# Attention kernel on one core: rows fetched as columns in one transfer a set, two additions split or moved, one reciprocal in halves

## Chip, cores, metric

The kernel runs on one core of a Trainium2 chip. The metric is the device time of one execution in microseconds (us): the median of several runs. Five engines are named here: PE (TensorE, matrix products), DVE (VectorE, elementwise work), ACT (ScalarE, copies, exponentials and sums with a bias), POOL (GpSimd, elementwise work beside DVE) and SP (SyncE, which issues most DMA transfers).

## What is computed

Eight images of 512 channels and 32 x 32 positions go through two attention blocks, all in float32:

```python
# layer 0: norm over 32 groups, 8 heads of 64 channels, softmax over positions
h = group_norm(x, norm_w, norm_b)
q, k, v = split(einsum('oc,bchw->bohw', qkv_w, h) + qkv_b)      # 8 heads
attn = softmax(einsum('bhnd,bhmd->bhnm', q, k) / sqrt(64))
o = einsum('bhnm,bhmd->bhnd', attn, v)
x = x + einsum('oc,bchw->bohw', proj_w, o) + proj_b

# layer 1: norm over the whole image, one head, softmax over 1024 positions
nf = norm(x) * gn_gamma + gn_beta
q, k, v = wq @ nf + bq, wk @ nf + bk, wv @ nf + bv
attn = softmax(q^T k * 512 ** -0.5)
out = v attn^T
x = x + wo @ out + bo
```

## The kernel before

Work goes image by image ("batch" 0 to 7), layer 0 and then layer 1, with the products of the next batch's layer 0 mixed in. Most 512- and 1024-wide products are Strassen products: `strassen` (from L640) and relatives compute a product of 2 x 2 blocks with seven block products. They need sums of blocks of both factors (S1 to S4 and T1 to T4), which DVE or POOL makes ahead of time, and sums of the results, which DVE adds from the PSUM banks as each is full. A bank that was not yet read can't be filled again, so an addition that is late keeps PE waiting. Some products apply the scheme twice (`twice` at L1503, `two_of` at L1795); their factors' sums have names with `_twice`.

Order. The order of PE, ACT and DVE is the order in which the program is written. Generators stand for products and give control back after each block product ("step"); `at_steps` runs them and calls given functions ("hooks") at numbered steps. So where a hook stands decides what is in front of what in DVE's queue. SP and POOL are ordered by the framework's scheduler. An engine works through its queue in order, and a DMA issue that has to wait holds everything behind it on the issuing engine.

Weights. Sums of weights that each batch needs are made in the first batch and stored to DRAM (`stored_...`, L247, L566), then loaded again by each later batch. Three large buffers (`wpool`) hold the weights in turn: the tile of v's weights (`w_v`, loaded at L220, its sums made at L195) takes the one that the product of wo and wv (`wvo`) had.

Vectors. The biases of the combined weights come out of PE as rows: class `Rows` (from about L730) multiplies vectors with weights into one PSUM bank, in which chunk cc of the input channels has its row at partition 32 cc (and a second row 16 further on, for sets of two). `store` (L749) copies the bank with ACT and stores all 128 rows to DRAM by SP; `fetch` (L755) loads each row back as a column of 128 partitions x 4, by one SP transfer for each row (8 for a set of two, 4 for a set of one); `add` (L765) adds the four chunks' columns on DVE (L769, L770). There are three sets: v and q, fetched ahead of batch 0 (L1926), and bias0, stored and fetched within batch 0 (L1031).

The places that the change touches, and what stands around them:

- `make_v` for batch 0 (PE L682): its first factor is `w_v`. ACT copies the first banks (L459) to `u_v`, DVE adds (L716). Before it PE makes `ps_k` (L667), which ACT copies with a bias (L697).
- The score blocks of layer 1. `twice("S4", ...)` and `twice("A22", ...)` run together, a step of one and a step of the other in turn. Each step is a group of four matmuls (L1512) into one of four banks, and a DVE addition `p<-ps_l,p` or `p<-ps_s,p` (L1522) that frees the bank. At step 3 a hook `c22(1)` (L1567) adds two whole score tiles of 128 x 1024 in SBUF (`with_p5`, L1565) and ACT takes their exponential (L1486). POOL adds up exponentials beside that (`add_up`, L1483), and then makes `B_p_twice` (L518).
- The values of layer 1. `four_of` for two chunks (PE L1676), then `two_of` (PE L1806, DVE L1812), with `done_values` behind each bank (DVE L1692, L1695). A hook at step 7 makes the four sums `S_v_twice` (`halve_v`, `sums_a`, L511) that `two_of` uses. POOL makes `A_v_twice` and DVE `B_p_twice` of other quarters.
- The end of layer 0 in the last batch. `done` in `project` (L1250 to L1287): behind the first banks of the two products, DVE takes a reciprocal of the last softmax sums (`one_over`, L847, 128 x 512) and divides (`divide`, L1018), then adds the other product's bank (L1273) and makes the remaining T sums (`combine2`, L1068). PE's `ps_p` (L667) needs the bank.

Of the kernel before, what the change touches and what calls it, by code (L numbers as in the profile page):

```python
# [37 lines left out]
FP = mybir.dt.float32  # L38
AF = mybir.ActivationFunctionType
ALU = mybir.AluOpType  # L40
# [6 lines left out]
P = 128  # L47
C = 512
NC = C // P
N = 1024  # L50
NT = N // P
HALF = 512
# [13 lines left out]
def two_attention_blocks(  # L66
# [18 lines left out]
    nc = tc.nc  # L85
    B = x.shape[0]

    const = ctx.enter_context(tc.tile_pool(name="const", bufs=1))
    tpool = ctx.enter_context(tc.tile_pool(name="t", bufs=36))
    wpool = ctx.enter_context(tc.tile_pool(name="w", bufs=3))  # L90
    dram = ctx.enter_context(tc.tile_pool(name="dram", bufs=1, space=bass.MemoryType.DRAM))
    upool = ctx.enter_context(tc.tile_pool(name="u", bufs=5))
    onepool = ctx.enter_context(tc.tile_pool(name="one", bufs=1))
    accpool = ctx.enter_context(tc.tile_pool(name="acc", bufs=2))
# [7 lines left out]
    def tile2(name):  # L102
        return tpool.tile([P, 2, HALF], FP, tag="t", name=name)
# [8 lines left out]
    def piece(ts, cc, half):  # L112

        return ts[cc // 2][half][:, cc % 2, :]
# [173 lines left out]
    def room(name, n=-1):  # L288

        return spares[n] if spares else banks("s", f"ps_{name}")[:, 0, :]  # L290
# [204 lines left out]
                quarter[f"{i + 1}{j + 1}"] = part[:, k, n * 2 * P : (n + 1) * 2 * P]  # L495
        return quarter

    def sums_a(q, t, engine=nc.vector):

        t = t if len(t.shape) == 2 else flat(t)  # L500
        n = t.shape[1] // 4
        for i in range(4):
            part = t[:, i * n : (i + 1) * n]
            if len(q["A11"].shape) == 3:
                part = part.rearrange("p (u o) -> p u o", u=2)
            q[f"S{i + 1}"] = part
        for i, x, y, op in [
            (1, "A21", "A22", ALU.add), (2, "S1", "A11", ALU.subtract),
            (3, "A11", "A21", ALU.subtract), (4, "A12", "S2", ALU.subtract),
        ]:  # L510
            engine.tensor_tensor(q[f"S{i}"], q[x], q[y], op)  # L511
        return q

    def sums_b(q, ts, engine=nc.vector):
# [217 lines left out]
    class Rows:  # L732
# [16 lines left out]
        def store(self):  # L749
            row = tile2(f"row_{self.name}")[:, 0, :]  # L750
            nc.scalar.copy(row, self.ps)
            self.rows = dram.tile([P, C], FP, tag=self.name, name=f"rows_{self.name}")
            nc.sync.dma_start(self.rows, row)

        def fetch(self):  # L755
            self.columns = const.tile(
                [P, self.n, NC, NC], FP, tag=f"c_{self.name}", name=f"c_{self.name}"
            )
            for i in range(self.n):
                for cc in range(NC):  # L760
                    nc.sync.dma_start(
                        self.columns[:, i, cc, :],
                        self.rows[cc * (P // NC) + i * (P // NC // 2)].rearrange("(o p) -> p o", p=P),
                    )

        def add(self, i, name):

            t, c = const.tile([P, NC], FP, tag=name, name=name), self.columns[:, i]
            nc.vector.tensor_tensor(c[:, :2, :], c[:, :2, :], c[:, 2:, :], ALU.add)  # L769
            nc.vector.tensor_tensor(t, c[:, 0, :], c[:, 1, :], ALU.add)  # L770
            made[name] = t
            return t
# [72 lines left out]
    def one_over(ps, name):  # L845
        inv = accpool.tile([P, HALF], FP, tag="inv", name=f"inv_{name}")[:, : ps.shape[1]]
        nc.vector.reciprocal(inv, ps)  # L847
        return inv
# [15 lines left out]
    def flat(t):  # L864
        return t.rearrange("p h n -> p (h n)")
# [76 lines left out]
    def layer0(bs, qs, ks, b, norm_next):  # L942
# [4 lines left out]
        hooks = {}  # L947
# [22 lines left out]
        accs, sums, invs, spreads = {}, {}, {}, {}  # L970
# [45 lines left out]
        def divide(pair, g, inv):  # L1016
            part = piece(os, pair, g)
            nc.vector.tensor_tensor(part, part, inv, ALU.mult)  # L1018

        units = [(pair, g, kt) for pair in ORDER for g in range(2) for kt in range(NT)]  # L1020
        ps = {}
# [5 lines left out]
        if b == 0:  # L1027
            w.finish()
            p0 = waiting[-1]

            def bias0():  # L1031
                rows = Rows([(bias_0, p0.moving)], 1, "bias0", room("bias0"))
                rows.store()
                rows.fetch()
                throughs[:] = [rows]

        hooks = {8: [lambda: score(0)], 9: [lambda: score(1)]}
# [15 lines left out]
        else:  # L1053
            hooks = {n + 10: more for n, more in hooks.items()}
            at_steps(pairs_qk_twice(w, twice_a[0], 1, bs, twice_b, qs, ks, b), hooks)
        last = norm_next is None
# [131 lines left out]
        for i in range(2, len(units) + 2):  # L1188
# [8 lines left out]
            name = f"0_{b}_{pair}_{g}"  # L1197
# [15 lines left out]
        if b == 0:  # L1213
            rows, = throughs
# [5 lines left out]
        if not last:  # L1220
# [3 lines left out]
            hooks = {  # L1224
                3: [lambda n=n: combine2(n, 0) for n in range(1, 5)],
                6: [lambda: folded(end)],
                12: [
                    lambda: sum_couple(couple, [room("sum", g) for g in range(2)]),
                    lambda: copy_couple(couple, 0), lambda: copy_couple(couple, 1), gather_couple,
                ],  # L1230
                14: [lambda: one_over_couple(couple, [nc.sync, nc.scalar])],
                16: [held_couple],
# [17 lines left out]
        def project(w, c):  # L1250
            def done(i, half, bank, u):
                chunk = c + 2 * i
                x = piece(xs, chunk, half)

                def add():
                    nc.vector.scalar_tensor_tensor(  # L1256
                        x, bank if u is None else u, bias[:, chunk : chunk + 1], x, ALU.add, ALU.add
                    )
                    due.append(lambda: norm.moments(chunk, half, i == half))
                    if (i, half, c) == (1, 0, 1):  # L1260
                        ready.halve("B21")


                first = last and i == half == 0
                if first and c == 0:
                    ps_sum, total = spares[0], tile_u(f"total_0_{b}")
                    add_keys(end, [1], ps_sum)
                    nc.scalar.copy(total, ps_sum)
                    combine1()
                    combine2(2, 0)  # L1270
                    combine2(3, 0)
                if u is not None:
                    nc.vector.tensor_tensor(u, bank, u, ALU.add)  # L1273
                if not first:
                    add()
                    return
                later.append(add)
                if c == 0:
                    invs[end] = one_over(total, f"0_{b}_{end}_1")
                    divide(end, 1, invs[end])  # L1280
                else:

                    held(flat(accs[end, 1]), f"acc_0_{b}_{end}", flat(accs[end, 1]))
                    for n, k in [(2, 1), (3, 1), (4, 0), (4, 1)]:
                        combine2(n, k)
                    for more in later:
                        more()  # L1287

            return strassen(by_channels(w, c, comb), done, f"p_0_{b}_{c}")

        w = next_weight().parts[0]
        hooks = {} if last else {2 * n - 3: [lambda n=n: combine2(n, 1)] for n in range(2, 5)}
# [31 lines left out]
    def attention1(xs, norm, ready, b, at_values):  # L1324

        last = b + 1 == B
# [144 lines left out]
        ps = [[[tile2(f"p_1_{b}_{j}{k}{i}") for i in range(2)] for k in range(2)] for j in range(2)]  # L1471
# [87 lines left out]
            done(1, 0)  # L1559
            yield  # L1560

        def with_p5(i, j, k):

            to, other = ps[j][k][i], ps[1][k][1] if i == 0 else ps[0][k][1]
            nc.vector.tensor_tensor(to, to, other, ALU.add)  # L1565

        def c22(k):  # L1567
            with_p5(1, 1, k)
            exp_of(ps[1][k][1])
# [58 lines left out]

        twice_v, twice_p = {}, {}

        def halve_v(name, engine):
            q = {
                f"A{i + 1}{j + 1}": v_parts[j][name][:, :, i * P : (i + 1) * P]
                for i in range(2) for j in range(2)
            }
            twice_v[name] = sums_a(q, tile2(f"{name}_v_twice_{b}"), engine)

        def halve_p(name, engine):
            q = {
                f"B{i + 1}{j + 1}": p_parts[i][name][:, :, j * 2 * P : (j + 1) * 2 * P]  # L1640
                for i in range(2) for j in range(2)
            }
            ts = [tile2(f"{name}_p_twice_{b}_{i}") for i in range(2)]
            sums = [t[:, i, :].rearrange("p (u q) -> p u q", u=2) for t in ts for i in range(2)]
            twice_p[name] = sums_b(q, sums, engine)

        if not last:
            halve_v("A12", nc.gpsimd)
        at_steps(
            together(  # L1650
                twice("S4", "B22", "oo", 0, 1, False, True), twice("A22", "T4", "ss", 1, 0, False, True)
            ),
            {3: [lambda: c22(1)], 5: [] if last else [lambda: halve_p("B22", nc.gpsimd)]},
        )

        for n in range(1, 5):
# [14 lines left out]
        invs, later = [], []  # L1671
# [87 lines left out]
        hooks = {n * 2 - 3: [lambda n=n: finish_values(n)] for n in range(2, 5)}  # L1759
# [64 lines left out]

        hooks[3].append(sums)
        hooks[6] = [lambda: halve_p("B21", nc.vector)]
        hooks[7] = [lambda: halve_v("S4", nc.vector)]
        for n, more in at_values.items():
            hooks.setdefault(n, []).extend(more)
        at_steps(in_turn(together(four_of(0), four_of(1)), two_of()), hooks)  # L1830
# [18 lines left out]
    made, throughs, over = {}, [], []  # L1849


    with tc.manual_schedule(engines={PE, ACT, DVE}):
# [71 lines left out]
        })  # L1924
        bs = combine.parts
        for rows in throughs:  # L1926
            rows.fetch()
        for b in range(B):
            if 0 < b < B - 1:
                ahead = [norm0(load_x(b + 1, nc.sync), b + 1)]  # L1930
# [430 lines left out]
```

## Time and profile before

| | |
|---|---|
| median of 3 runs | 2820.49 us (2820.47 to 2820.8) |
| the profiled execution | 2819.71 us |
| its span, first to last instruction | 2818.0 us |
| granted TensorE clock, mean | 0.999 |
| DMA traffic | 246.45 MB, mean 87 GB/s |

How to read the profile. All durations come from one profiled execution, whose own time is 1.7 us above its span. The page gives the busy time of each engine, the chain of work that ended last, and groups of equal instructions. "PEld" is PE's weight load, which runs beside matmuls. The waits view lists, for each engine and line, what ended its idle time: the total in us, how often, and the longest. The timeline gives one line for an instruction or a run of them: start in us, duration, engine, line, operation, output<-inputs, the shape, the count, and in brackets the idle time before it with what ended it. A "SPq" or "ACTq" line is the issue of a DMA by that engine, not the transfer. A time over a group (x2) covers all of the group.

### The profile page before, as it was taken

To read this page: it belongs to the slowest core of one execution; us is meant where nothing else is said; L and a number is where in the kernel's file an instruction comes from. 1 tells how busy PE (TensorE), PEld (TensorE's weight loads), DVE (VectorE), ACT (ScalarE), POOL (GpSimd) and SP (SyncE) were. 2 spreads that over 40 slices of the span, in tenths; PEclk is the share of its full clock that TensorE was granted. 3 is DMA by queue.
4 is the path that set the end of the run, shared out by engine and by line. 5 is a ranking of instruction groups with operands and counts; after the bars stand their busy time and mean duration, and the time that the engine had idled before them with its cause. 6 is when DMAs were issued, how large, how long until landed. Compare 5 with 4: busy or idle time off the path is not lost.

```text
span 2818.0 us, 39402 instructions
## 1 busy us (share of the span) xinstructions
PE 2805.0 (100%) x15688; PEld 1586.0 (56%) x15688; DVE 2113.7 (75%) x2891; ACT 1172.3 (42%) x1761; POOL 377.7 (13%) x388
## 2 busy tenths in 40 slices
PE   9999999999999999999999999999999999999999
PEld 5535765357653576435764466734667346673375
DVE  5777697766977678776787767777777777767877
ACT  3364224643246332563325533255332653326622
POOL 0001220012100230002400024000240002400021
PEclk9999999999999999999999999999999999999999
DMA  7524132231313313233131331312313132121001
GB/s 252 201 53 132 42 123 79 75 107 63 114 64 87 105 53 112 68 91 114 67 107 43 91 124 57 109 50 85 123 56 108 50 104 104 64 80 62 25 16 39
DMA packets 83575, 246.45 MB, mean 87 GB/s; under 512 B 21784, under 2 KB 22584, under 8 KB 76984
## 3 DMA queue, kind: packets, MB, share of 16 engines
q1 hardware_dynamic: 73768, 209.75, 22.9%
q10 hardware_dynamic: 9616, 34.11, 3.8%
q8 instruction: 125, 2.05, 0.3%
q14 instruction: 66, 0.54, 0.1%
HBM read 186.97 MB, written 33.03 MB: 78 GB/s over the span
## 4 chain that ended last, share of the span: by engine, by line
PE 92%; DVE 6%; issue 1%; DMA 1%; SPq 0%; ACT 0%; POOL 0%; DVEq 0%; ACTq 0%; POOLq 0%
PE s L979 15%; PE ps_o L998 15%; PE ps_v L682 7%; PE ps_o L1676 7%; PE ps_p L667 7%; PE ps_l_qk L904 5%; PE ps_l L1512 4%; PE ps_s L1495 4%; PE ps_s_qk L897 4%; PE ps_l_v L682 3%; PE ps_l_q L667 3%; PE ps_s L1512 3%; PE ps_o_qk L897 3%; PE ps_s_v L925 2%; PE ps_s_q L1370 2%; PE ps_s_two L1806 2%
## 5 line engine op out<-in xcount | busy, mean ns | idle before, releaser
L833 ACT ACTIVATE p<-s 128x1024 f32<-128x1024 f32 x512 | 523.9, 1025 | 328.9 <-PE s L979 322.8
L835 DVE TENSOR_TENSOR acc<-acc,p 128x1024 f32<-128x1024 f32 x384 | 469.1, 1222 | 101.0 <-ACT p L833 92.5
L998 PE MATMUL ps_o<-p,v 64*64 64x512 f32 x4096 | 528.7, 589 | 0.0
L979 PE MATMUL s<-c_q,c_k 64*64 64x512 f32 x3584 | 465.1, 590 | 0.0
L998 PEld LDWEIGHTS ps_o<-p,v 64*64 64x64 f32 x4096 | 156.6, 133 | 282.8 <-issue 278.3
L979 PEld LDWEIGHTS s<-c_q,c_k 64*64 64x64 f32 x3584 | 134.7, 133 | 253.2 <-issue 236.1
L528 POOL TENSOR_TENSOR B_twice<-x 128x512 f32<-128x512 f32 x16 | 20.4, 1274 | 1352.1 <-DVE x L1256 1351.9
L1676 PE MATMUL ps_o<-t_p,s_v 128*128 128x512 f32 x384 | 168.2, 594 | 0.0
L835 DVE TENSOR_TENSOR acc<-p,p 128x1024 f32<-128x1024 f32 x64 | 78.2, 1223 | 79.4 <-ACT p L833 79.4
L1486 ACT ACTIVATE p<-p,factor 128x512 f32<-128x512 f32 (+1 forms) x112 | 85.3, 780 | 116.1 <-DVE p L1522 91.4
L1500 ACT COPY p<-ps_s 128x512 f32<-128x512 f32 x96 | 53.1, 588 | 174.4 <-PE ps_s L1495 174.4
L1676 PEld LDWEIGHTS ps_o<-t_p,s_v 128*128 128x128 f32 x384 | 72.3, 190 | 91.3 <-issue 89.2
L1522 DVE TENSOR_TENSOR p<-ps_l,p 128x512 f32<-128x512 f32 x136 | 89.8, 682 | 40.0 <-PE ps_l L1512 39.7
L459 ACT COPY u_v<-ps_v 128x512 f32<-128x512 f32 x48 | 28.1, 586 | 210.1 <-PE ps_v L682 191.2
L667 PE MATMUL ps_p<-t_p,w_p 128*128 128x512 f32 x256 | 112.7, 592 | 0.6 <-DVE u_p L1273 0.6
L1522 DVE TENSOR_TENSOR p<-ps_s,p 128x512 f32<-128x512 f32 x112 | 74.8, 684 | 37.7 <-PE ps_s L1512 37.7
L682 PE MATMUL ps_v<-w_v,t_again 128*128 128x256 f32 x448 | 99.0, 379 | 0.0
L373 POOL TENSOR_TENSOR rstd<-rstd,minus_half 128x4 f32<-128x4 f32 (+1 forms) x16 | 12.8, 800 | 605.5 <-DVE rstd L372 605.5
L682 PE MATMUL ps_v<-w_v,x 128*128 128x256 f32 x384 | 88.6, 385 | 3.4 <-DMA w_v<-in_s_v 3.4
L682 PEld LDWEIGHTS ps_v<-w_v,t_again 128*128 128x128 f32 x448 | 85.1, 190 | 11.6
L667 PE MATMUL ps_p<-o,w_p 128*128 128x512 f32 x192 | 86.7, 593 | 0.0
L667 PEld LDWEIGHTS ps_p<-t_p,w_p 128*128 128x128 f32 x256 | 48.6, 190 | 62.2 <-issue 58.4
(508 smaller groups left out, 5148.7 us busy)
## 6 DMA issues: line engine op xcount, KB each, us to landing
x<-in_x SPq DMA_DIRECT2D x92, 512.0 KB, 6.4
w_qk<-stored_qk SPq DMA_DIRECT2D x14, 1792.0 KB, 7.1
w_wqk<-stored_wqk SPq DMA_DIRECT2D x8, 1792.0 KB, 7.2
fold<-acc SPq DMA_DIRECT2D x56, 256.0 KB, 3.1
qk_twice<-stored_qk_twice ACTq DMA_DIRECT2D x28, 512.0 KB, 6.1
w_wvo<-stored_wvo SPq DMA_DIRECT2D x8, 1792.0 KB, 8.3
out<-x SPq DMA_DIRECT2D x28, 512.0 KB, 4.7
w_v<-stored_v SPq DMA_DIRECT2D x7, 1792.0 KB, 7.5
```

Source lines behind the costliest of these rows:

```text
L667: nc.tensor.matmul(bank, w[a][:, k, c * P : (c + 1) * P], bs[b][:, k, :], start=fresh and k == 0, stop=k == 1, skip_group_check=True,)
L682: nc.tensor.matmul(bank[:, u * 2 * P : (u + 1) * 2 * P], bs[b][:, k, n * P : (n + 1) * P], w[a][:, k, :], start=fresh and u == k == 0, sto ...
L833: nc.scalar.activation(p, s, AF.Exp, scale=factor)
L835: nc.vector.tensor_tensor(acc, first, p, ALU.add)
L897: nc.tensor.matmul(bank[:, i * 2 * P : (i + 1) * 2 * P], parts[a][x], twice_b[v][y], start=start and i == 0, stop=True, skip_group_check=True,
L904: nc.tensor.matmul(bank, of(i, a)[:, k, :], bs[v][:, k, :], start=start and k == 0, stop=k == 1, skip_group_check=True,)
L979: nc.tensor.matmul(s[cols, j, :], ks[pair][k0 // HALF][rows, k0 % HALF : k0 % HALF + HD], qs[pair][g][rows, :], start=True, stop=True,)
L998: nc.tensor.matmul(o[cols, half, :], vs[kt][rows, c0 : c0 + HD], p[rows, j, :], start=kt == 0, stop=kt == NT - 1,)
L1495: nc.tensor.matmul(bank, bs[v][:, k, t * P : (t + 1) * P], q_parts[a][:, k, :], start=a == "A11" and k == 0, stop=k == 1, skip_group_check ...
L1512: nc.tensor.matmul(bank[:, u * 2 * P : (u + 1) * 2 * P], v[y][:, u * P : (u + 1) * P], a[x], start=start and u == 0, stop=True, skip_group ...
L1522: nc.vector.tensor_tensor(at(r, t), bank, at(r, t), ALU.add)
L1676: nc.tensor.matmul(bank, v_parts[kt // 2][a][:, kt % 2, c * P : (c + 1) * P], p_parts[kt // 2][b][:, kt % 2, cols], start=fresh and kt == ...
```

## The change

Four things are changed. Nothing else is: PE's order and POOL's order are the same as before.

1. `Rows.store` writes only the 8 (or 4) rows that are used, and `fetch` brings them all to columns with one transfer of 128 x 32 (or 128 x 16) single elements. The sets v and q are fetched by ACT (their two issues stand behind the copy of `k`, L697, and ahead of the first copy to `u_v`), bias0 by SP. On SP, sixteen issues ahead of and around the load of `w_v` are gone: the load now stands between the two stores of `wvo_twice`.
2. The sum at `c22(1)` is made in two halves of 128 x 512: one at step 3, one at step 4, with the exponential of the whole behind the second. On DVE one bank's addition (L1522) comes between them.
3. The four sums `S_v_twice` are made in pairs at steps 8 and 10 in place of step 7: on DVE they stand two divisions (L1692) and more further back. The last batch has no such sums.
4. The last batch's reciprocal is made in two halves of 128 x 256, the second behind the other product's addition (L1273), with the division behind it.

```diff
@@ -495,7 +495,7 @@
                 quarter[f"{i + 1}{j + 1}"] = part[:, k, n * 2 * P : (n + 1) * 2 * P]
         return quarter
 
-    def sums_a(q, t, engine=nc.vector):
+    def sums_a(q, t, engine=nc.vector, made=range(1, 5)):
 
         t = t if len(t.shape) == 2 else flat(t)
         n = t.shape[1] // 4
@@ -508,7 +508,8 @@
             (1, "A21", "A22", ALU.add), (2, "S1", "A11", ALU.subtract),
             (3, "A11", "A21", ALU.subtract), (4, "A12", "S2", ALU.subtract),
         ]:
-            engine.tensor_tensor(q[f"S{i}"], q[x], q[y], op)
+            if i in made:
+                engine.tensor_tensor(q[f"S{i}"], q[x], q[y], op)
         return q
 
     def sums_b(q, ts, engine=nc.vector):
@@ -749,23 +750,23 @@
         def store(self):
             row = tile2(f"row_{self.name}")[:, 0, :]
             nc.scalar.copy(row, self.ps)
-            self.rows = dram.tile([P, C], FP, tag=self.name, name=f"rows_{self.name}")
-            nc.sync.dma_start(self.rows, row)
-
-        def fetch(self):
+            n = NC * self.n
+            self.rows = dram.tile([n, C], FP, tag=self.name, name=f"rows_{self.name}")
+            nc.sync.dma_start(self.rows, row[0 : P : P // n, :])
+
+        def fetch(self, queue):
             self.columns = const.tile(
-                [P, self.n, NC, NC], FP, tag=f"c_{self.name}", name=f"c_{self.name}"
+                [P, NC * self.n, NC], FP, tag=f"c_{self.name}", name=f"c_{self.name}"
             )
-            for i in range(self.n):
-                for cc in range(NC):
-                    nc.sync.dma_start(
-                        self.columns[:, i, cc, :],
-                        self.rows[cc * (P // NC) + i * (P // NC // 2)].rearrange("(o p) -> p o", p=P),
-                    )
+            queue.dma_start(
+                self.columns.rearrange("p n o -> p (n o)"),
+                self.rows.rearrange("n (o p) -> p (n o)", p=P),
+            )
 
         def add(self, i, name):
 
-            t, c = const.tile([P, NC], FP, tag=name, name=name), self.columns[:, i]
+            t = const.tile([P, NC], FP, tag=name, name=name)
+            c = self.columns.rearrange("p (c n) o -> p c n o", n=self.n)[:, :, i, :]
             nc.vector.tensor_tensor(c[:, :2, :], c[:, :2, :], c[:, 2:, :], ALU.add)
             nc.vector.tensor_tensor(t, c[:, 0, :], c[:, 1, :], ALU.add)
             made[name] = t
@@ -1031,7 +1032,7 @@
             def bias0():
                 rows = Rows([(bias_0, p0.moving)], 1, "bias0", room("bias0"))
                 rows.store()
-                rows.fetch()
+                rows.fetch(nc.sync)
                 throughs[:] = [rows]
 
         hooks = {8: [lambda: score(0)], 9: [lambda: score(1)]}
@@ -1275,10 +1276,15 @@
                     add()
                     return
                 later.append(add)
+                low, high = slice(0, 2 * P), slice(2 * P, HALF)
                 if c == 0:
-                    invs[end] = one_over(total, f"0_{b}_{end}_1")
-                    divide(end, 1, invs[end])
+                    inv = accpool.tile([P, HALF], FP, tag="inv", name=f"inv_0_{b}_{end}_1")
+                    invs[end], invs["of"] = inv, total
+                    nc.vector.reciprocal(inv[:, low], total[:, low])
                 else:
+                    inv, total = invs[end], invs.pop("of")
+                    nc.vector.reciprocal(inv[:, high], total[:, high])
+                    divide(end, 1, inv)
 
                     held(flat(accs[end, 1]), f"acc_0_{b}_{end}", flat(accs[end, 1]))
                     for n, k in [(2, 1), (3, 1), (4, 0), (4, 1)]:
@@ -1559,10 +1565,10 @@
             done(1, 0)
             yield
 
-        def with_p5(i, j, k):
+        def with_p5(i, j, k, us=slice(0, 2)):
 
             to, other = ps[j][k][i], ps[1][k][1] if i == 0 else ps[0][k][1]
-            nc.vector.tensor_tensor(to, to, other, ALU.add)
+            nc.vector.tensor_tensor(to[:, us, :], to[:, us, :], other[:, us, :], ALU.add)
 
         def c22(k):
             with_p5(1, 1, k)
@@ -1628,12 +1634,14 @@
 
         twice_v, twice_p = {}, {}
 
-        def halve_v(name, engine):
+        def halve_v(name, engine, made=range(1, 5)):
             q = {
                 f"A{i + 1}{j + 1}": v_parts[j][name][:, :, i * P : (i + 1) * P]
                 for i in range(2) for j in range(2)
             }
-            twice_v[name] = sums_a(q, tile2(f"{name}_v_twice_{b}"), engine)
+            if made[0] == 1:
+                twice_v[name, "tile"] = tile2(f"{name}_v_twice_{b}")
+            twice_v[name] = sums_a(q, twice_v[name, "tile"], engine, made)
 
         def halve_p(name, engine):
             q = {
@@ -1644,13 +1652,17 @@
             sums = [t[:, i, :].rearrange("p (u q) -> p u q", u=2) for t in ts for i in range(2)]
             twice_p[name] = sums_b(q, sums, engine)
 
+        def c22_end():
+            with_p5(1, 1, 1, slice(1, 2))
+            exp_of(ps[1][1][1])
+
         if not last:
             halve_v("A12", nc.gpsimd)
         at_steps(
             together(
                 twice("S4", "B22", "oo", 0, 1, False, True), twice("A22", "T4", "ss", 1, 0, False, True)
             ),
-            {3: [lambda: c22(1)], 5: [] if last else [lambda: halve_p("B22", nc.gpsimd)]},
+            {3: [lambda: with_p5(1, 1, 1, slice(0, 1))], 4: [c22_end], 5: [] if last else [lambda: halve_p("B22", nc.gpsimd)]},
         )
 
         for n in range(1, 5):
@@ -1824,7 +1836,8 @@
 
         hooks[3].append(sums)
         hooks[6] = [lambda: halve_p("B21", nc.vector)]
-        hooks[7] = [lambda: halve_v("S4", nc.vector)]
+        hooks[8] = [lambda: halve_v("S4", nc.vector, [1, 2])]
+        hooks[10] = [lambda: halve_v("S4", nc.vector, [3, 4])]
         for n, more in at_values.items():
             hooks.setdefault(n, []).extend(more)
         at_steps(in_turn(together(four_of(0), four_of(1)), two_of()), hooks)
@@ -1924,7 +1937,7 @@
         })
         bs = combine.parts
         for rows in throughs:
-            rows.fetch()
+            rows.fetch(nc.scalar)
         for b in range(B):
             if 0 < b < B - 1:
                 ahead = [norm0(load_x(b + 1, nc.sync), b + 1)]
```

## Prediction

> **What bounds the kernel now.** I read the page first: busy shares and the chain that ended last.
>
> ```profile
> PE 2805.0 (100%) x15688; PEld 1586.0 (56%) x15688; DVE 2113.7 (75%) x2891; ACT 1172.3 (42%) x1761; POOL 377.7 (13%) x388
> PE 92%; DVE 6%; issue 1%; DMA 1%; SPq 0%; ACT 0%; POOL 0%; DVEq 0%; ACTq 0%; POOLq 0%
> ```
>
> TensorE (PE) is busy for the whole span of 2818.0 us, at a granted clock of 0.999. So an edit pays only where PE waits. The waits view, cut to PE and its weight load (columns: total us, times, longest), gives the candidates:
>
> ```profile
> PE ps_v L682 <- DMA w_v<-in_s_v: 3.4, 1, 3.4
> PE ps_l L1512 <- DVE p L1522: 1.2, 7, 0.2
> PEld ps_l L1512 <- DVE p L1522: 6.9, 14, 0.6
> PEld ps_s_two L1806 <- DVE o L1692: 6.8, 7, 1.0
> ```
>
> One stall at the start, and two small ones in each of the seven batches that are not the last. Each touches a part of the change. The timeline of each place says what ended it (columns: start, duration, engine, line; in brackets the idle time before). The start:
>
> ```profile
> 46.39 0.38 SPq L753 DMA_DIRECT2D rows_q<-row_q  x1
> ...
> 53.38 2.57 SPq L761 DMA_DIRECT2D c_q<-rows_q  x5
> ...
> 56.55 0.43 SPq L761 DMA_DIRECT2D c_q<-rows_q  x1
> ...
> 57.09 0.85 SPq L220 DMA_DIRECT2D w_v<-in_s_v  x1
> ...
> 64.03 8.83 PE L682 MATMUL ps_v<-w_v,x 128*128 128x256 f32 x32 [3.38 <-DMA w_v<-in_s_v]
> ```
>
> SyncE (SP) waits until 53.38 for rows_q to reach DRAM, issues column fetches, and only then w_v, for which PE stands. The end of a score bank (batch 1 as the example):
>
> ```profile
> 702.98 3.50 POOL L1483 TENSOR_TENSOR acc<-acc,p 128x512 f32<-128x512 f32 x2
> ...
> 703.25 2.09 DVE L1565 TENSOR_TENSOR p<-p,p 128x1024 f32<-128x1024 f32 x1
> ...
> 705.26 1.27 DVE L1522 TENSOR_TENSOR p<-ps_l,p 128x512 f32<-128x512 f32 x2
> ...
> 705.99 1.13 PE L1512 MATMUL ps_l<-S_twice,B_twice 128*128 128x256 f32 x4 [0.17 <-DVE p L1522]
> ```
>
> VectorE (DVE) spends 2.09 us on one sum, and the bank's add comes behind it.
>
> **What the Trainium skill says.** "SBUF — State Buffer", section "Who interferes with whom": a DVE instruction with two SBUF inputs contends with a GpSimd (POOL) instruction that reads SBUF, over a shared port that is an exclusive lock; one with a single SBUF input does not. The trace agrees: the same 128x1024 sum takes 1.25 us where POOL is idle (at 699.68) and 2.09 here; POOL's adds take 1.27 free and 2.14 when DVE is in front; L1522, whose first input is PSUM, keeps 0.68 throughout. "DMA: Bandwidth & Descriptors", "Rules for kernel authors": a strided last dimension lowers to one descriptor per element. So one transfer a set does not reduce the elements: 8 x 512 before, 4096 after. Here 4-byte packets take 9 ns each (4305 of them from 52.0 to 65.2), 2.2 us of all 16 engines for 4096. The same page, "Issuing engines are not separate DMA queues": another issuing engine saves sequencer time only. That is what matters here: SP's time. "TensorE: Matmul & The Clock Gate", "What's actually happening": after an idle window the array runs at half clock. The trace agrees: a clock of 0.50 from 66 to 68 us, after the start's stall, and nowhere near it later.
>
> **Part A, fetches moved off SP.** SP loses 16 issues and the wait for rows_q. In the new order w_v follows the first store of wvo_twice; it needs the completion of the store of wvo (issued 45.97, landed 52.8; w_v takes its buffer) and DVE's wvo_twice sums, done at 51.9. So w_v is issued at 52.8 to 53.0 in place of 57.09, and lands after the 6.8 us that it took before (the trace shows no reason for more: the elements leave its window): 59.7. PE's last matmul ahead of it, the second of a pair at 59.63, makes the next due at 60.49. It started at 64.03: 3.54 lost. Then, at the lowered clock, the first 32 matmuls took 8.66 us (64.03 to 72.69) where 32 x 0.2146 = 6.87: 1.79 lost. Removed: 5.3 us. Next late: DVE's chain from the landing to the first v sum (L716) took 6.93 us (64.01 to 70.94); from 59.7 it ends at 66.6, and PE needs the sums S of w_v at 60.49 + 6.87 = 67.36. It holds, with 0.7 to spare. If w_v landed as late as before, the gain would be nothing.
>
> What ScalarE (ACT) gets: two issues of 4096 elements behind the copy of k (58.97 + 0.69 = 59.66); rows_v and rows_q have landed by then. Behind them in ACT's queue are the copies of ps_v (L459), the first due at 62.3 but without a reader before L716 at 66.6, so that both issues may take some 6.4 us together for nothing (ACT free at 66.1). Their price is not in the trace. Low end: a 128-row store costs 0.38, a 512-element fetch 0.51 (2.57 over 5), so 0.13 for 384 elements, and 0.38 + 3968 x 0.00034 = 1.7 for 4096. Middle: eight times a fetch with its gap (0.55), 4.4. High end: eight times the slowest, 1.51 (at 58.97, with w_v's packets in front), 12.1. A gain is excluded, ACT having issued nothing here before. I take 1.7 to 3: below 6.4 for two, hidden. The columns' reader (L769) is at 90.8. bias0's single fetch stays on SP, four issues (2.03 us at 119.18) become one, needed near 240: nothing. The stores shrink from 128 rows to 8 or 4, with the same wait behind them: nothing.
>
> **Part B, the sum in front of a bank in halves (7 batches).** Before: the next PE group was due at 705.66, started at 705.99, and its second matmul came 0.10 late (weight load exposed): 0.43 lost. After: half one waits for POOL's first add (to 704.25) and takes about 0.54 (half of 1.08), to 704.8. POOL's second add, ready since 704.33, takes the lock and ends at 704.8 + 1.14 = 705.94. The bank's add (PSUM input, no lock) runs 704.7 to 705.4: PE is on time, 0.43 gained. But half two stands in DVE's queue from 705.3, is shut out until 705.94, ends at 706.49, and the next bank's add behind it ends at 707.09 in place of 706.53. PE wants that bank at 706.52, starts at 707.14 with 0.10 of exposed load: 0.72 lost. Net +0.29 x 7 = +2.0. Bounds: no lock in the way, -0.43 x 7 = -3.0; POOL's next instruction (1.27) in front of half two as well, +1.57 x 7 = +11.0. The last batch shows no stall here, POOL idle: nothing.
>
> **Part C, four sums S4 moved (7 batches).** Columns as above:
>
> ```profile
> 744.41 0.42 DVE L511 TENSOR_TENSOR S_v_twice<-s_v 128x256 f32<-128x256 f32 x1
> ...
> 745.88 0.74 DVE L1692 SCALAR_TENSOR_TENSOR o<-ps_o,rstd,inv 128x512 f32<-128x512 f32 x1
> ...
> 746.68 1.13 PE L1806 MATMUL ps_s_two<-p,c_v 128*128 128x256 f32 x4
> ```
>
> The sixteen matmuls before, at 0.4294 each from 739.51, make PE due at 746.38; it starts at 746.68 plus 0.10 of load: 0.40. Without the four sums (744.41 to 745.95) L1692 runs at 744.5 to 745.2. Two sums follow at once, needed from 749.8; two fall in DVE's idle 0.98 at 750.43, needed after 753. All hidden: -0.40 x 7 = -2.8. If that cover failed, at most their 1.5 us came back.
>
> **Part D, last reciprocal in halves.** At the end of layer 0 of the last batch:
>
> ```profile
> 2652.73 3.34 DVE L847 RECIPROCAL inv<-total 128x512 f32<-128x512 f32 x1
> ...
> 2656.71 0.68 DVE L1273 TENSOR_TENSOR u_p<-ps_p,u_p 128x512 f32<-128x512 f32 x1
> ...
> 2657.45 2.84 PE L667 MATMUL ps_p<-t_p,w_p 128*128 128x512 f32 x6 [0.65 <-DVE u_p L1273]
> ```
>
> PE was due at 2654.92 + 4 x 0.43 = 2656.64: 0.81 lost, with 0.1 of load. A 128x256 reciprocal takes 1.75 (the row of that shape), so the add L1273 runs once the bank is full, 2655.15 to 2655.85: PE on time. The second half and the division then end at 2658.15; the T2 sum behind them ends at 2658.8, PE wants it at 2658.4 for its first half of channels, 2659.2 for this one: 0 to 0.4 given back. Net -0.5 to -0.9, say -0.85.
>
> **Sum.** -5.3 + 2.0 - 2.8 - 0.85 = -6.95, against the profiled execution: 2819.71, 1.7 of it outside the span. That gives 2812.8. The median of the runs stands 0.78 above that execution: 2813.5.
>
> **Rivals.**
> - Half two isn't shut out: 2813.5 - 2.0 - 3.0 = 2808.5. For it: the stall before was only 0.33. Against it: POOL's second add waits already (its 2.14).
> - ACT is held by its issues at the middle price: 8.8 us, free at 68.5 where 66.1 would do; 2.4 lost, and up to 1.8 more if the clock falls again. 2816 to 2817.7. For it: one 512-element issue took 1.51. Against: most took 0.5.
> - The other side, the same mechanism at the high price: 2 x 12.1 = 24.2, ACT free at 83.9, 17.8 lost and 1.8 of clock: 2813.5 + 19.6 = 2833. It decides from 6.95 - 1.8 + 6.4 = 11.5 us for both issues, 5.8 each, on.
> - The transfer is hidden no better: w_v waits for something else, and lands after 63; -5.3 is gone: 2818.8.
>
> **Chances.** Likeliest case 0.50 (2813.5, own range 2811.5 to 2815.5), half two free 0.20, ACT held in the middle 0.16, w_v still late 0.07, the other side 0.07. 0.2%, about what a measurement of this kernel can tell from no change, is 5.64 us: faster means below 2814.85. Of the likeliest case about 0.37 lies there, with 0.20 from the free half: 0.57. Slower by 0.2% (above 2826.1) is the other side alone, 0.07; the rest, 0.36, is the same. The range runs from below the free half to the end of the held one, 2808.0 to 2817.8, which leaves out 0.14 and some edges.
>
> **What would show it.** Right: no stall at L682 for w_v, and a full clock there; the wait of ps_s_two on L1692 gone; in the seven batches a stall one group later, on the second L1522, with half two at about 1.1 us in place of 0.6; the wait at L1273 gone. Wrong: ACT's first L459 copy after 66; POOL's L518 add in front of half two; a new wait at PE in steps 12 to 15 of the value products on L511.

## The result and the profile after

The changed kernel takes 2813.74 us (median of 12 runs, 2813.14 to 2815.01) against 2820.44 for the kernel before (2818.78 to 2821.03, 12 runs): ratio 0.9977, 95% interval 0.9969 to 0.9986. The forecast was 2813.5. The profiled execution took 2814.33, its span 2812.6 against 2818.0.

The page's busy line and the chain of work that ended last:

```profile
PE 2800.5 (100%) x15688; PEld 1585.1 (56%) x15688; DVE 2115.3 (75%) x2900; ACT 1171.6 (42%) x1761; POOL 376.9 (13%) x388
PE 97%; DVE 2%; issue 1%; POOL 0%; DVEq 0%; POOLq 0%
```

PE still fills the span; the DMA share of the chain is gone, and DVE's fell from 6% to 2%. PE's own waits, the whole list:

```profile
PE ps_l L1518 <- DVE p L1528: 5.2, 7, 0.8
PE ps_warm L1872 <- POOL in_sample L164: 1.2, 1, 1.2
```

Three of four waits are gone: w_v, L1692's hold on ps_s_two (a wait of PEld, whose list no longer has it), and the one at L1273 (now L1274). The fourth, at the score banks, grew from 1.2 to 5.2 us. So one part of the change lost time.

Since PE's order is the same, the nth of its 15688 matmuls can be compared between the two traces: where the difference of their starts jumps, time was won or lost. The jumps, in us:

| place | predicted | measured |
|---|---|---|
| first loads, before 7 us | - | -0.25 |
| v products of batch 0: stall for w_v, then the clock | -3.54 - 1.79 | -5.30 in all |
| first score bank, each of 7 batches | -0.43 | -0.45 |
| second score bank, each of 7 | +0.72 | +0.98 |
| ps_s_two, each of 7 | -0.40 | -0.41 |
| ps_p, last batch | -0.85 | -0.91 |

With the sevens this makes -5.62; the last matmul came 5.57 us earlier (2806.64 against 2812.22). The start, in the timeline of after:

```profile
52.13 0.33 SPq L220 DMA_DIRECT2D w_v<-in_s_v  x1
...
58.66 0.69 DVE L195 TENSOR_TENSOR w_v<-rest_v,w_v 128x512 f32<-128x512 f32 x1 [0.91 <-DMA w_v<-in_s_v]
...
58.78 0.39 ACTq L761 DMA_DIRECT2D c_v<-rows_v  x1
59.26 2.97 ACTq L761 DMA_DIRECT2D c_q<-rows_q  x1
...
60.23 7.07 PE L683 MATMUL ps_v<-w_v,x 128*128 128x256 f32 x32
...
62.32 0.59 ACT L459 COPY u_v<-ps_v 128x512 f32<-128x512 f32 x1 [2.92 <-DVE qk_twice L512]
```

w_v is issued 5 us earlier and has landed when its first reader, DVE, takes it at 58.66; PE goes on without a gap, and 32 matmuls take 7.07 in place of 8.83. ACT's two issues end at 62.23, and the copy behind them starts at once. (Its bracket counts ACT's issuing as idle time and names the last event seen from another engine, so DVE is not what held it.) The score banks (batch 1):

```profile
697.54 2.96 POOL L1489 TENSOR_TENSOR acc<-acc,p 128x512 f32<-128x512 f32 x2
...
697.81 1.55 DVE L1571 TENSOR_TENSOR p<-p,p 128x512 f32<-128x512 f32 x1
...
699.29 0.68 DVE L1528 TENSOR_TENSOR p<-ps_l,p 128x512 f32<-128x512 f32 x1
...
699.89 1.16 DVE L1571 TENSOR_TENSOR p<-p,p 128x512 f32<-128x512 f32 x1
...
701.15 0.69 DVE L1528 TENSOR_TENSOR p<-ps_l,p 128x512 f32<-128x512 f32 x1
...
701.99 1.10 PE L1518 MATMUL ps_l<-A_twice,T_twice 128*128 128x256 f32 x4 [0.73 <-DVE p L1528]
```

Both halves are as long as they are because POOL's two additions, one ahead of each, hold the port: half one 1.55, half two 1.16. The first bank is on time; the second waits. The S4 sums, now behind L1704 (L1692 before) and ahead of nothing that PE needs, and the end of layer 0:

```profile
739.52 0.75 DVE L1704 SCALAR_TENSOR_TENSOR o<-ps_o,rstd,inv 128x512 f32<-128x512 f32 x1
...
740.97 0.42 DVE L512 TENSOR_TENSOR S_v_twice<-s_v 128x256 f32<-128x256 f32 x1
...
741.48 1.03 PE L1818 MATMUL ps_s_two<-p,c_v 128*128 128x256 f32 x4
```

```profile
2648.06 1.74 DVE L1283 RECIPROCAL inv<-total 128x256 f32<-128x256 f32 x1
...
2650.26 4.03 PE L668 MATMUL ps_p<-t_p,w_p 128*128 128x512 f32 x9
2650.53 0.69 DVE L1274 TENSOR_TENSOR u_p<-ps_p,u_p 128x512 f32<-128x512 f32 x1 [0.72 <-PE ps_p L668]
2651.13 1.74 DVE L1286 RECIPROCAL inv<-total 128x256 f32<-128x256 f32 x1
```

DVE now waits 0.72 for PE's bank where PE waited for DVE, and nine matmuls of ps_p run without a break.

### The profile page after: what moved, and what is told of

Its sections match the earlier page's. It is cut to its first block, busy times and chain, and to the rows that moved or that the text cites. A ratio compares the mean times of both kernels' runs of the same rounds, so it can differ in the third digit from the quotient of the medians.

```text
span 2812.6 us, 39373 instructions
## 1 busy us (share of the span) xinstructions
PE 2800.5 (100%) x15688; PEld 1585.1 (56%) x15688; DVE 2115.3 (75%) x2900; ACT 1171.6 (42%) x1761; POOL 376.9 (13%) x388
## 4 chain that ended last, share of the span: by engine, by line
PE 97%; DVE 2%; issue 1%; POOL 0%; DVEq 0%; POOLq 0%
PE s L980 16%; PE ps_o L999 16%; PE ps_o L1688 10%; PE ps_v L683 7%; PE ps_p L668 7%; PE ps_l_qk L905 5%; PE ps_l L1518 4%; PE ps_s L1501 4%; PE ps_s_qk L898 4%; PE ps_l_v L683 3%; PE ps_l_q L668 3%; PE ps_s L1518 3%; PE ps_o_qk L898 3%; PE ps_s_v L926 2%; PE ps_s_q L1376 2%; PE ps_s_two L1818 2%
```

## The experiments

In each, "before" is the kernel before on the same chip. Its medians were 2820.44 beside the changed kernel and 2819.44 to 2820.71 below, so medians of kernels that ran on different chips compare to about 1 us. Gains at a named place are jumps between matmuls, each from one profiled execution.

**The sum whole again.** In the changed kernel:

```diff
-            {3: [lambda: with_p5(1, 1, 1, slice(0, 1))], 4: [c22_end], 5: ...},
+            {3: [lambda: c22(1)], 5: ...},
```

> The changed kernel with the sum ahead of the bank whole again, at step 3. Theory (the split costs, since POOL's second addition holds the port between the halves): the seven stalls on the second bank, 0.97 us each against the kernel before's 0.45, go back to 0.45: 0.5 x 7 = 3.7 us less than the changed kernel, about 2810.0 us. Rival (the 3.7 us missing in batches came from the moved S4 sums, not from the split): no change, 2813.7 us, and the stall stays where it was.

Measured: 2809.69 us (2809.49 to 2811.36, 5 runs; before 2820.71), ratio 0.9962 (0.9948 to 0.9975). PE's waits for the score banks are the old ones:

```profile
PE ps_l L1518 <- DVE p L1528: 1.1, 7, 0.2
```

Between matmuls the whole sum gains 3.8 us on the changed kernel, so the split lost more than the 2.0 forecast for it, and this is the rest of the change without its one losing part.

**The split alone.** The kernel before with that hook in halves (the diff above the other way round, and `with_p5` with its slice).

> The kernel before with the sum in halves alone. Theory: seven stalls move one group on and grow from 0.45 to 0.97 us: 3.7 us more than before, about 2824.1 us. Rival (the split gains by itself, and the changed kernel loses the gain to another of its parts): 3.0 us less, 2817.4.

Measured: 2824.45 us (2821.86 to 2825.74, 13 runs; before 2820.71), ratio 1.0012 (1.0004 to 1.0021): 3.7 us slower, the theory's number. In each batch -0.45 at the first bank and about +0.98 at the second, as in the changed kernel.

**The fetches alone.** The kernel before with `Rows.store` and `fetch` changed and `throughs` fetched by ACT.

> The kernel before with the fetches alone changed (one transfer a set, issued by ACT). Theory: the stall for w_v (3.54) and the lowered clock behind it (1.79) go, nothing else: 5.3 us less than before, about 2815.1 us. Rival (the clock fell for another reason than the stall): 3.5 us less, 2816.9, with a clock near 0.5 still somewhere between 60 and 70 us.

Measured: 2814.05 us (2813.17 to 2814.38, 9 runs; before 2820.71), ratio 0.9976 (0.9966 to 0.9986). In the trace this kernel gains at the v products what the changed one does, to 0.01 us, and the clock stays at 1.00 in both, so the rival falls. 6.7 us in the medians is more than the 5.3 of the profiled pair. The traces show part of why: three profiled executions with the old fetches (before, the split alone, the additions alone below) lost 5.30, 5.46 and 6.06 us at this place.

**The other two alone.** The kernel before with the S4 sums moved and the reciprocal in halves.

> The kernel before with the four S4 sums moved and the last reciprocal in halves, nothing else. Theory (their stalls are independent of the rest): 0.41 x 7 for ps_s_two and 0.91 for ps_p, 3.8 us less than before, about 2816.7 us. Rival (what they gain comes back behind them, once the other parts don't shift the work): less than 2 us.

Measured: 2816.32 us (2814.96 to 2818.05, 21 runs; before 2820.37), ratio 0.9985 (0.9979 to 0.9992): 4.05 us less. The theory holds: 0.41 in each of seven batches and 0.91 at ps_p, the same as in the changed kernel. The two parts were not run apart; the places of the jumps tell them apart.

**One transfer, but issued by SP.** What gained at the start: fewer issues, or leaving SP?

```diff
         for rows in throughs:
-            rows.fetch(nc.scalar)
+            rows.fetch(nc.sync)
```

> The changed kernel with its one transfer a set, but issued by SP ahead of w_v, as the old fetches were. Theory (what held w_v was the number of issues and SP's wait for rows_q together; one issue into an empty queue costs 0.4): rows_q lands near 52.8, the issue of w_v follows near 53.6, it lands between 59.8 and 62 with the 4096 elements beside it: a stall of 0 to 1.8 us, 2813.7 to 2816.5 us. Rival (the fetches have to leave SP): w_v is issued near 57 as before, the whole 5.3 us come back, 2819 us.

Measured: 2816.04 us (2815.08 to 2817.41, 21 runs; before 2820.71), ratio 0.9984 (0.9977 to 0.999). That is within the theory's range, near its upper end. In the trace 2.8 us of the 5.3 come back: 2.1 at the stall for w_v, 0.7 behind it, where DVE's sums are late for PE. (By the medians 2.0 to 2.3 come back.) SP's queue and PE:

```profile
51.46 0.37 SPq L761 DMA_DIRECT2D c_q<-rows_q  x1
51.92 2.33 SPq L567 DMA_DIRECT2D stored_wvo_twice<-wvo_twice  x1
54.35 0.37 SPq L220 DMA_DIRECT2D w_v<-in_s_v  x1
...
61.32 7.14 PE L683 MATMUL ps_v<-w_v,x 128*128 128x256 f32 x32 [1.83 <-DMA w_v<-in_s_v]
```

The issue of 4096 elements itself takes 0.37; it is the next issue on the same queue that takes 2.33. I had priced the first and not the second. Counted from the same matmul, w_v is issued 3.1 us later than in the changed kernel and its first reader starts 3.5 later. So about half of the gain is fewer issues, and half is that the queue which fills is not SP's. Its table of windows has one more thing (PEclk is the third number from the end):

```profile
62.00:64.00 2.00, 2.00 (x11) 1.74 (x11) 2.00 (x4) 0.59 (x1) 0.00 (x0) 1.00 0.03 8
```

After a stall of 2.0 us the clock stayed at 1.00. After the 3.5 of before it fell to 0.50.

**Sixteen transfers on ACT.** In the changed kernel, one transfer for each row, by the same queue:

```diff
-            queue.dma_start(
-                self.columns.rearrange("p n o -> p (n o)"),
-                self.rows.rearrange("n (o p) -> p (n o)", p=P),
-            )
+            for n in range(NC * self.n):
+                queue.dma_start(self.columns[:, n, :], self.rows[n].rearrange("(o p) -> p o", p=P))
```

> The changed kernel with the old sixteen transfers of 512 elements, issued by ACT in the place of the two. SP's order stays the changed one. Theory (the gain at the start is SP's time alone): w_v lands as early as in the changed kernel, no stall for it. ACT issues for 16 x 0.5 to 0.55 us, 8.0 to 8.8, and is free near 67.4 where 66.0 would do: 1 to 2.5 us lost in the first v product, 2815 to 2816.3 us. Rival (the number of transfers is what matters): most of the 5.3 us come back, 2818 us or more.

Measured: 2823.22 us (2821.16 to 2824.43, 21 runs; before 2819.44), ratio 1.0012 (1.0006 to 1.0019): 9.5 us above the changed kernel's median (10.5 with each set against its own before). The number lies in the rival's range, but not for its reason: w_v was issued at 51.68 and there was no stall for it, which the rival needs. The theory's place was right and its price wrong:

```profile
58.43 8.54 ACTq L762 DMA_DIRECT2D c_v<-rows_v  x8
...
67.01 6.08 ACTq L762 DMA_DIRECT2D c_q<-rows_q  x8
...
73.19 1.07 ACT L459 COPY u_v<-ps_v 128x512 f32<-128x512 f32 x2 [14.13 <-DMA c_q<-rows_q]
...
74.55 2.08 PE L683 MATMUL ps_v<-w_v,t 128*128 128x256 f32 x4 [7.60 <-DVE v L717]
...
76.00:78.00 2.00, 2.00 (x6) 1.64 (x5) 1.97 (x7) 0.00 (x0) 0.00 (x0) 0.50 0.32 129
```

ACT was held until 73.1, PE stood 7.8 us for the copies behind, and then ran at a clock of 0.50 for 5 us (3.1 more). Ten of the sixteen issues took 0.39 to 0.55 and one 0.81, three from 62.6 to 67.0 took 1.37 to 1.54, and two others 1.72 (at 59.4) and 1.91 (at 70.6). From 62.6 to 66 the store of w_v (1.8 MB in packets of 14336 bytes) was under way, and few 4-byte packets moved: 52 on ACT's queue from 64 to 66, against 2412 from 66 to 68. The store moved 53 packets in the first of these stretches: one for one, as if the two queues took turns packet by packet. From PE's stall, ACT would have done at 65.3: 73.1 - 7.8.

**Each set fetched twice.** In the changed kernel:

```diff
-            queue.dma_start(
-                self.columns.rearrange("p n o -> p (n o)"),
-                self.rows.rearrange("n (o p) -> p (n o)", p=P),
-            )
+            again = dram.tile([P, NC * self.n * NC], FP, tag=f"again_{self.name}", name=...)
+            for to in [self.columns.rearrange("p n o -> p (n o)"), again]:
+                queue.dma_start(to, self.rows.rearrange("n (o p) -> p (n o)", p=P))
```

> The changed kernel with each set's transfer issued twice (the second into an unused place in DRAM), so ACT issues four transfers of 4096 elements here; for bias0 SP issues two. Theory (an issue of 4096 elements costs what the queue needs to drain the one ahead of it, 3.0 us, and the first one 0.4): ACT is held 0.4 + 3 x 3.0 = 9.4 us, to 68.2, where 66.0 would do: 2.2 us lost, and up to 1.8 more if the clock falls: 2816 to 2817.7 us. Rival (issues on ACT are hidden whatever they take, for the copies behind them have time): as the changed kernel, 2813.7 us.

Measured: 2861.53 us (2860.57 to 2863.63, 5 runs; before 2819.44), ratio 1.0152 (1.0138 to 1.0166). Both numbers are missed. The four issues and the copy behind them:

```profile
58.33 0.39 ACTq L763 DMA_DIRECT2D c_v<-rows_v  x1
58.76 3.12 ACTq L763 DMA_DIRECT2D again_v<-rows_v  x1
...
61.91 10.67 ACTq L763 DMA_DIRECT2D c_q<-rows_q  x1
...
72.63 27.04 ACTq L763 DMA_DIRECT2D again_q<-rows_q  x1
99.76 1.07 ACT L459 COPY u_v<-ps_v 128x512 f32<-128x512 f32 x2 [40.81 <-DMA c_q<-rows_q]
```

It is no clean doubling: the first copy's 4-byte packets took 23 ns each from 66 to 68 us and 177 from 68 to 80, against 9 for those to SBUF. What it does show: an issue lasts until enough of the packets ahead of it have gone. It took 0.39 with none ahead, 3.12 behind a set for SBUF, and 10.67 behind the first copy to DRAM, whose packets moved only from 66.15 on, when the store of w_v was nearly through. Nothing on ACT hides that past about 65 us. The rival "hidden whatever they take" falls.

**POOL out of the way, with halves and whole.** Is it the port, or DVE's own order, that makes the split lose? Both kernels give POOL an order written by hand in which it waits for the sum's exponential, and put its two additions off (shown in part; the rest passes `order` on):

```diff
-    with tc.manual_schedule(engines={PE, ACT, DVE}):
+    with tc.manual_schedule(engines={PE, ACT, DVE, mybir.EngineType.Pool}):
...
-                        add_up(j, t, i)
+                        if (j, t) == (0, 0) and not last:
+                            put_off.append(lambda: add_up(0, 0, 0))
+                        else:
+                            add_up(j, t, i)
...
-            twice_p[name] = sums_b(q, sums, engine)
+            twice_p[name] = sums_b(q, sums, engine, (3, 1, 2, 4) if engine is nc.gpsimd else (1, 2, 3, 4))
+            if engine is nc.gpsimd:
+                for more in put_off:
+                    more()
...
-            2: [lambda: ready.halve("T1"), norm.both_halves],
+            2: [norm.both_halves, lambda: ready.halve("T1")],
```

> The changed kernel (sum in halves), with POOL's order written by hand so that POOL stands still there: its first addition of that stretch is one that needs the exponential of the sum, and the two additions that ran beside the halves come after four others. Theory (the port's lock is the cause): both halves take about 0.6 us, the second bank's add is on time, the seven stalls of 0.97 us go: 6.8 us less than the changed kernel, about 2806.9 us. Rival (DVE's own order is the cause: half two and its wait stand in front of the second bank's add whatever POOL does): a stall of 0.5 or more stays at the second bank, 2810 us or more.

> The same order on POOL, with the sum whole again at step 3. Theory: without the lock the sum takes 1.25 us, ends 0.8 earlier than before, and the first bank's add is on time: the seven stalls of 0.45 go, 3.15 us less than with the sum whole and POOL as it was (2809.7), about 2806.5 us, the same as with halves. Rival (a sum of 128x1024 is too long for that place even alone, so that the halves are needed): a stall at the first bank stays, and this is 1 to 3 us slower than the halves with the same order on POOL.

Measured: 2810.79 us with halves (2810.39 to 2811.62, 7 runs; before 2819.44; ratio 0.9971, 0.9959 to 0.9982), and 2809.09 whole (2808.83 to 2809.59, 5 runs; ratio 0.9965, 0.9951 to 0.9978). On the question the theory holds in both. With halves:

```profile
696.73 0.67 DVE L1576 TENSOR_TENSOR p<-p,p 128x512 f32<-128x512 f32 x1
...
697.33 0.68 DVE L1530 TENSOR_TENSOR p<-ps_l,p 128x512 f32<-128x512 f32 x1
...
697.93 0.67 DVE L1576 TENSOR_TENSOR p<-p,p 128x512 f32<-128x512 f32 x1
...
698.71 0.69 DVE L1530 TENSOR_TENSOR p<-ps_l,p 128x512 f32<-128x512 f32 x1
```

And whole:

```profile
696.41 1.21 DVE L1576 TENSOR_TENSOR p<-p,p 128x1024 f32<-128x1024 f32 x1
```

The halves take 0.67 (1.55 and 1.16 with POOL beside them), the whole sum 1.21 in place of 2.09, and in both the stall at the banks is gone. Neither time was met, because the accumulator that was put off came late, and PE waited for what is made of it:

```profile
PE ps_o L1696 <- ACT held_sum L846: 4.2, 7, 0.6
```

That is a new wait of my own making: 0.67 us lost in each batch, and at the sums of the accumulator 0.36 more with halves, 0.09 more whole. Beside it, POOL's order by hand gained 0.41 a batch at two places outside this stretch (0.25 at ps_l of the S1 product, 0.16 at ps_l_q). The traces show the port there too: in batch 1 of the changed kernel a DVE sum of 128 x 1024 in front of each of these banks took 2.14 us (at 685.24) and 1.84 (at 620.17) with POOL's instructions beside it. With POOL by hand, in the next two kernels as well, each took 1.22.

**POOL by hand, nothing put off.** So the additions stay early: the same two lines on POOL's order (`manual_schedule` and hook 2), without `put_off` and without `order`. In the program's order they stand ahead of the A_v_twice sums.

> The changed kernel with the sum whole at step 3 and POOL in the order in which the program is written, nothing put off: the two additions of the accumulator now stand ahead of the four A_v_twice sums, so that what runs beside DVE's sum are instructions of 128x256 (0.73 us) and not of 128x512. Theory (the lock decides, and its cost is the length of the one instruction that holds it): the sum waits at most 0.7 and ends some 0.6 us earlier than before, the first bank's add is on time, and the accumulator isn't late as it was with the additions put off: the seven stalls of 0.45 go, and the 0.36 per batch that POOL's order gained elsewhere in the last two runs stays: 2809.7 - 3.15 - 2.5 = about 2804.0 us. Rival (the late accumulator comes with any order by hand): 0.6 x 7 = 4 us come back, 2808 us.

> The same order on POOL, with the sum in halves as in the changed kernel. Theory: half two meets an instruction of POOL too, at most 0.73 us long in place of 1.14: a stall of 0 to 0.5 us a batch at the second bank, so 0 to 3.5 us slower than with the sum whole, 2804 to 2807.5 us. Rival (halves are as good as the whole once POOL's pieces are small): within 0.3 us of the whole.

Measured: whole, 2804.05 us (2803.29 to 2804.49, 5 runs; before 2820.37), ratio 0.9941 (0.9927 to 0.9955). In halves, 2804.16 us (2803.46 to 2804.94, 5 runs), ratio 0.9942 (0.9929 to 0.9956). The first is the theory's number; of the second the rival holds, within 0.3 us. Both beat the changed kernel and the kernel before. PE's waits of the first, the whole list, and its stretch on POOL and DVE:

```profile
PE ps_warm L1872 <- POOL in_sample L164: 1.2, 1, 1.2
```

```profile
692.52 3.72 POOL L1489 TENSOR_TENSOR acc<-acc,p 128x512 f32<-128x512 f32 x2 [0.53 <-ACT p L1492]
...
696.06 1.27 DVE L1571 TENSOR_TENSOR p<-p,p 128x1024 f32<-128x1024 f32 x1
...
696.20 1.71 POOL L512 TENSOR_TENSOR A_v_twice<-c_v,c_v 128x256 f32<-128x256 f32 x1
...
697.25 1.27 DVE L1528 TENSOR_TENSOR p<-ps_l,p 128x512 f32<-128x512 f32 x2
```

DVE's sum came first, in every batch, and took 1.27, and it is POOL that waited (1.71 for an instruction that takes 0.73 free). The list has no wait of PE for that. Once the lock is out of DVE's way, halves and whole differ by 0.1 us, less than either kernel's spread: the split has nothing left to do.

## Why the prediction was right, and where not

**The start (A): mechanism and size right, -5.30 against -5.3.** w_v was issued at 52.13 (52.8 to 53.0 predicted; it waited for the store of wvo, issued at 45.72. Its landing is not in this trace; in the kernel with sixteen transfers on ACT that store took 6.25 us, in the kernel before 6.77, and w_v followed at once) and was in by 58.66 (59.7 predicted). DVE's chain reached the first v sum at 65.59, with no wait at PE. The price of the issues was an estimate per element, 1.7 to 3 each; measured 0.39 and 2.97. The sum of 3.36 is just under the low end of what I took for two (3.4 to 6), but not for my reason, so that this price came out is luck: the first 4096 elements cost ACT next to nothing, and the second issue waited for a queue that had to drain. The limit of 66.1 for ACT was near: 65.3 by the kernel with sixteen transfers. The cover is thinner than I wrote: the second issue ended at 62.23, just when the store of w_v began to move and 4-byte packets stopped (its own elements moved only from 66.15 on, most of them by 69). That the rival "ACT held" did not come true hangs on that, as I read it.

**The split (B): mechanism right, the term of +2.0 mis-sized; it was +3.7.** Half two ended at 701.04, to 0.02 us where the working had it, shifted by PE's lead of 5.43. What failed is the next line of the step: "the next bank's add behind it ends at 707.09". I let that add begin 0.08 ahead of half two's end, as DVE's instructions otherwise overlap. It began 0.10 after it, and PE 0.15 after its end. In the trace a wait of DVE for an event stands between them, 0.04 us after half two's end, and in the kernel before one stands 0.04 after the whole sum's end, where the first bank's add hid it. The event is one of DVE's own, and PE had filled the bank by 698.7, so the add waits for an earlier DVE instruction. I read it as waiting to overwrite a tile that half two reads; no run took that wait by itself away. The working had PE 0.05 behind the add's end; why it was 0.15 stays open. Term by term: 0.98 lost at the second bank in place of 0.72, 0.45 gained at the first in place of 0.43.

**The moved sums (C): -2.87 against -2.8. The reciprocal (D): -0.91 against -0.85**, nothing given back at T2.

**The sum.** By its own steps the profiled pair moved by -5.4 (span), not -6.95; the medians moved by -6.7. So the closeness of 2813.5 to 2813.74 is partly luck, two errors that cancel: 1.7 us too little for the split, and 1.3 by which the medians lie further apart than the profiled pair (before's median is 0.73 above its profiled execution, the changed kernel's 0.59 below). The traces show two sources for the second: the loads before 7 us shift whole executions by up to 1.2 us, and the old stall for w_v ranges from 5.30 to 6.06. Whether these make up all of the 1.3 stays open.

Of the rivals, "half two isn't shut out" is refuted for this kernel (1.16 us) and came true only with POOL by hand. The other side did not happen, but its mechanism is real: held until 73.1 by sixteen transfers, ACT cost 10.9 us in all.

## What to carry to other kernels

Ahead of splitting an instruction that is too long, look for what makes it long. Here a 1.2 us sum took 2.1 because another engine held the port, and splitting it gave that engine a second turn; to order the other engine was worth 5.6 us (by the jumps 3.0 at these banks and 2.9 at two places with the same lock) where the split lost 3.7. And a DMA of 4096 elements cost its issuer 0.4 us: the one who pays is whatever is issued next on that queue, so count the queue's next customer, and the large transfers that will run beside it.

## What the runs showed of the hardware

- A DVE sum of 128 x 1024 with both inputs in SBUF took 2.08 to 2.16 us behind POOL's 128 x 512 sums, and 1.21 to 1.27 with POOL out of the way or behind it. A POOL sum of 128 x 256 took 0.73, and 1.71 behind DVE's.
- 4096 elements of 4 bytes were issued in 0.37 to 0.39 us into an empty queue, 512 in 0.37 to 0.39. The next issue on that queue took 2.3 to 3.1.
- Beside a 1.8 MB store in 14336-byte packets, 4-byte packets of another queue all but stopped: 52 in 2 us, with 53 of the store, against 2412 in the next 2.
- 4-byte packets from DRAM took 9 ns to SBUF; in one run, with DRAM as the target, 23 at first and 177 on average in the 12 us that followed.
- A stall of PE of 2.0 us left the clock at 1.00; those of 3.5 and 7.8 us were followed by 0.50.
